# A decoder block with cross-attention and MLP on one core: proj's bias added to the residual by VectorE instead of GpSimd

## The chip, the cores and the metric

The kernel runs on one core of one Trainium2 chip, as one launch. The metric is the device time of that launch in microseconds (us); of several runs the median counts. TensorE is PE in the rows (its weight loads are PEld), VectorE is DVE, ScalarE is ACT, GpSimd is POOL, and SyncE, which only starts transfers here, is SP.

## The reference

Four batches (B = 4) of 512 rows (L) with D = 512 columns, 16 heads, and an MLP 4 x 512 = 2048 wide. Everything is float32.

```python
residual = hidden_states
x = layer_norm(hidden_states, ln1_w, ln1_b)
q = x @ q_w + q_b; k = enc @ k_w + k_b; v = enc @ v_w + v_b      # per head
attn = softmax(where(mask, q @ k.T * scale, min))
out = (attn @ v) @ cproj_w + cproj_b
hidden = out + residual
y = gelu(layer_norm(hidden, ln2_w, ln2_b) @ fc_w + fc_b)
return hidden + (y @ proj_w + proj_b)
```

The last line is what the change touches: `proj_b`, a row of 512 numbers, is added to every row of `hidden`.

## The kernel before, in words

The program is one long list of short steps. A string, `ORDER`, names them in the order in which their instructions are written (`name:batch:part`); each mention of a token runs its generator up to the next `yield`. An engine carries out its own instructions strictly in that written order and waits, at each one, for what it needs from other engines and transfers. Nothing reorders them later, so the string decides what stands behind what in each engine's queue.

The run has two halves. Up to about 545 us attention and MLP steps of the batches are mixed. The rest is the last MLP work of batch 3 and then, for batches 0 to 3, the projection `y @ proj_w`. Each matrix product here is done with sums of blocks so that it takes seven block products instead of eight (and mostly once more inside each of these): blocks are added and subtracted beforehand by VectorE, and results are added up afterwards.

In the projection the steps are these:

- `la` loads gelu's output of a batch from DRAM, where it was parked, into a slot of the tile `swap` (or the two staging tiles `st`), and `gs` (VectorE, lines 331 and 334) forms differences and sums of slots.
- `xs` (VectorE) forms four smaller sums of a slot in the tile `ext`; two such sets alternate. `pt` and `ps` do the same for proj's weights (tiles `pbt`, `ptt`, `mix`, `ys`, `ws`).
- `P` (TensorE, line 637) multiplies them into PSUM banks `acc` and `sc`; `pj` copies the banks into a row tile `xn` (ScalarE, line 663) and adds the second bank (VectorE, `xn<-sc,xn`).
- `hd` (SyncE) loads the parked `hidden` of a batch from the DRAM tensor `xa` in four tiles of 128 rows, t = 0 to 3. For batches 0 and 2 they go to the last slot of `swap`, for batches 1 and 3 to `yT`.
- `pb` (line 738) adds the bias row to the four tiles, one at each mention: `swap<-swap,row` or `yT<-yT,row`, 128 partitions by 512. `row` is proj's bias, loaded once and copied to all partitions.
- `J` adds the results of the products onto the tiles. Mostly this is a transfer that adds as it writes (issued by GpSimd, line 849, `swap<-xn` or `yT<-xn`), for two results of the last batch an addition by VectorE. `so` stores the finished tiles.

For batch 0 the `pb` mentions stand among the last MLP steps, for batches 1 to 3 among the projection steps of the batch before.

Of the kernel before, what the change touches and what calls it, by code (L numbers as in the profile page):

```python
# [241 lines left out]
def xattn_block(ctx: ExitStack, tc: tile.TileContext, x, encT, mask, q_w, k_w, v_w, c_w, w_fc, p_w, vecs, rows, out):  # L242
    nc = tc.nc
# [12 lines left out]
    row = const.tile([P, 2, D], F32, tag="row", name="row")  # L256
# [73 lines left out]
    def add(engine, o, x0, x1):  # L330
        engine.tensor_tensor(o, x0, x1, ALU.add)  # L331
# [403 lines left out]
    def p_bias(b):  # L735
        for t in range(NT):
            o = hids[b % 2][:, t]
            add(nc.gpsimd, o, o, row[:, 0, :])
            yield

    def g_sums(b, n):
# [150 lines left out]
    for _ in range(WARM):  # L892
# [6 lines left out]
        "wk": load_k, "wq": load_q, "wv": load_v, "le": load_enc, "lc": lambda: load(wc, c_w),  # L899
        "pk": prep_k, "q": prep_q, "es": e_sums, "k": kv("k"), "v": kv("v"), "ks": kv_sums("k"), "vs": kv_sums("v"),  # L900
        "kj": k_join, "vj": v_join, "vb": v_bias, "lr": load_row, "pb": p_bias, "qb": q_bias, "m": make_mb,
        "u": scores, "x": exps, "r": turn, "d": stay, "e": exchange, "a": attend,
        "lx": lambda b: load_x((1, b)), "lh": lambda b: load_x((2, b)), "cb": c_bias, "c": cproj,
# [59 lines left out]
```

## Time and profile before

| | us |
|---|---|
| median of 3 runs | 780.06 |
| the 3 runs | 779.04, 780.06, 782.16 |
| time of the profiled execution | 780.34 |
| its span, first to last instruction | 778.3 |
| PE busy in the span | 757.7 (97%) |
| DVE busy | 635.0 (82%) |
| POOL busy | 426.6 (55%) |
| ACT busy | 404.4 (52%) |
| mean granted clock of PE | 0.991 |

The span is what the rows of the trace cover, counted from its first instruction; about 2 us of the execution's time lie around it. A busy share is a mean over both halves. The granted clock is the share of full speed that the chip gave TensorE.

### The profile page before, as it was taken

The numbers are of one execution on the slowest core, as the hardware profiler recorded it, in microseconds if no ns is written. First come the engines' busy times: TensorE is split into PE (matmuls) and PEld (weight loads), VectorE is DVE, ScalarE is ACT, GpSimd is POOL, SyncE is SP. The second block draws the span as 40 slices with busy tenths as digits, with TensorE's granted clock in tenths as the row PEclk, the third lists the DMA queues.
The fourth block names the chain that finished last, engine by engine and source line by source line (L and its number), as shares of the span: only waits on it lengthen the run. The fifth ranks groups of instructions, "written<-read, shape, count | busy, mean of one in ns | idle before, by whom it ended". The sixth has DMA issues, their size and how long they took to land.

```text
span 778.3 us, 14426 instructions
## 1 busy us (share of the span) xinstructions
PE 757.7 (97%) x4990; PEld 555.0 (71%) x4990; DVE 635.0 (82%) x1230; ACT 404.4 (52%) x978; POOL 426.6 (55%) x467
## 2 busy tenths in 40 slices
PE   7999999999999999999999999999999999979898
PEld 4665555556665566766566776758888999979897
DVE  3899999999798799998679696528789797987882
ACT  1668675648879578767847797612333211111110
POOL 3367757956686498556767658726204133431441
PEclk8999999999999999999999999999999999999999
DMA  7578988867876886768778787786545668786456
GB/s 274 169 202 217 252 215 198 236 181 209 242 200 184 247 222 176 221 185 221 210 193 244 228 262 223 205 311 259 156 135 144 218 155 230 136 230 167 109 90 137
DMA packets 69447, 157.48 MB, mean 202 GB/s; under 512 B 11600, under 2 KB 24272, under 8 KB 67712
## 3 DMA queue, kind: packets, MB, share of 16 engines
q1 hardware_dynamic: 54272, 126.72, 56.7%
q0 software_dynamic: 14960, 29.82, 15.2%
q8 instruction: 40, 0.66, 0.4%
q14 instruction: 31, 0.25, 0.1%
q10 hardware_dynamic: 144, 0.02, 0.0%
HBM read 69.23 MB, written 25.17 MB: 121 GB/s over the span
## 4 chain that ended last, share of the span: by engine, by line
PE 69%; DVE 12%; issue 5%; DMA 5%; POOL 4%; ACT 2%; SPq 2%; DVEq 0%; POOLq 0%; ACTq 0%
PE acc L637 27%; PE sc L637 9%; PE acc L467 9%; PE sc L524 7%; PE acc L516 6%; PE acc L582 5%; PE acc L402 5%; SPq L328 2%; DVE ext L334 2%; DVE ptt L532 2%; DVE swap L543 1%; PE acc L370 1%; POOL swap L560 1%; DMA swap<-swap 1%; PE acc L438 1%
## 5 line engine op out<-in xcount | busy, mean ns | idle before, releaser
L535 ACT ACTIVATE ptt<-ptt,mn 128x512 f32<-128x512 f32 x256 | 182.9, 716 | 53.2 <-DVE mn L532 52.1
L532 DVE CUSTOM_DVE_ANT_0 ptt<-sc,mix 128x512 f32<-128x512 f32 x256 | 164.9, 678 | 21.0 <-PE sc L524 17.0
L560 POOL COPY swap<-swap 32x1088 f32<-32x1088 f32 x128 | 140.5, 1098 | 56.4 <-DVE swap L553 45.8
L663 ACT COPY st<-acc 128x256 f32<-128x256 f32 x128 | 46.0, 367 | 103.2 <-PE acc L637 84.3
L663 ACT COPY xn<-acc 128x128 f32<-128x128 f32 x100 | 23.5, 269 | 136.5 <-PE acc L637 134.5
L543 DVE STREAM_TRANSPOSE swap<-ptt 128x1024 f32<-128x1024 f32 x64 | 79.0, 1235 | 9.1 <-DMA swap<-swap 4.5
L524 PE MATMUL sc<-pbt 32*128 32x512 f32 x512 | 78.0, 640 | 0.0
L550 DVE STREAM_TRANSPOSE swap<-ptt 128x1024 f32<-128x1024 f32 x64 | 77.8, 1218 | 0.0
L691 POOL DMA_DIRECT2D gd<-st x32 | 23.7, 741 | 90.7 <-ACT st L689 56.9
L637 PE MATMUL acc<-ys,ws 128*128 128x256 f32 x256 | 65.4, 386 | 0.8 <-ACT st L663 0.7
L582 PE MATMUL acc<-swap,mix 128*32 128x256 f32 x1024 | 61.3, 382 | 0.3 <-ACT ptt L535 0.3
L637 PEld LDWEIGHTS acc<-ys,ws 128*128 128x128 f32 x256 | 46.7, 190 | 18.2 <-issue 4.8
L637 PE MATMUL acc<-yT,pbt 128*128 128x256 f32 x240 | 58.2, 385 | 0.4 <-ACT yT L380 0.4
L516 PE MATMUL acc<-ext,ptt 128*128 128x512 f32 x128 | 58.4, 599 | 0.0
L402 PE MATMUL acc<-mix 128*128 128x512 f32 x128 | 58.1, 598 | 0.0
L637 PEld LDWEIGHTS acc<-yT,pbt 128*128 128x128 f32 x240 | 44.2, 190 | 15.1 <-issue 4.3
L582 PEld LDWEIGHTS acc<-swap,mix 128*32 128x32 f32 x1024 | 30.5, 109 | 30.9 <-issue 10.9
L849 POOL DMA_DIRECT2D swap<-xn x18 | 22.4, 1423 | 50.0 <-ACT xn L663 18.9
L535 ACT ACTIVATION_READ_ACCUMULATOR ptt<-ptt,mn 128x1 f32 x256 | 48.4, 189 | 0.0
L689 ACT ACTIVATE st<-st,vec 128x512 f32<-128x512 f32 x64 | 43.6, 717 | 3.1 <-DVE st L331 2.7
L516 PEld LDWEIGHTS acc<-ext,ptt 128*128 128x128 f32 x128 | 23.5, 190 | 28.6 <-issue 23.5
L402 PEld LDWEIGHTS acc<-mix 128*128 128x128 f32 x128 | 23.6, 190 | 28.4 <-issue 26.3
(154 smaller groups left out, 1609.4 us busy)
## 6 DMA issues: line engine op xcount, KB each, us to landing
swap<-swap SPq DMA_DIRECT2D x384, 136.0 KB, 3.3
gd<-st POOLq DMA_DIRECT2D x32, 512.0 KB, 4.1
swap<-gd SPq DMA_DIRECT2D x12, 1024.0 KB, 5.4
pbt<-fc_w_dram SPq DMA_DIRECT2D x40, 256.0 KB, 3.7
xn<-x_dram SPq DMA_DIRECT2D x32, 256.0 KB, 4.6
ext<-fc_w_dram SPq DMA_DIRECT2D x24, 256.0 KB, 3.0
swap<-xn POOLq DMA_DIRECT2D x18, 256.0 KB, 4.9
ptt<-k_w_dram SPq DMA_DIRECT2D x16, 256.0 KB, 3.5
```

The lines of the kernel that those rows point to most:

```text
L402: nc.tensor.matmul(acc, oT[:, g, ts(t, P)], wc[:, g, :], start=(g == 0), stop=(g == NG - 1))
L467: nc.tensor.matmul(out_, i, j, start=(k + t == 0 and not more), stop=(k == 1), skip_group_check=more or t > 0)
L516: nc.tensor.matmul(acc, S["wq", w][:, d, :], xT[:, d, :], start=(d == 0), stop=(d == ND - 1))
L524: nc.tensor.matmul(sc[h], S["qT", w][r, ts(qt, P)], S["kT", w][r, :], start=True, stop=True)
L532: nc.vector.tensor_tensor_reduce(out=s, in0=sc[h], in1=mb, scale=1.0, scalar=FMAX, op0=ALU.add, op1=ALU.min, accum_out=mn)
L535: nc.scalar.activation(s, s, AF.Exp, bias=mn, scale=-1.0, accum_out=S["sums", w][:, qt, h : h + 1])
L543: nc.vector.transpose(*two_heads[0])
L550: nc.vector.transpose(*two_heads[1])
L560: nc.gpsimd.tensor_copy(pT[ts(i, HD), i], tb[ts(i, HD), i])
L582: nc.tensor.matmul(av[ts(h, HD), : 2 * P].rearrange(shape, **kw), v[:, t, ts(h, HD)], p[t][h], start=(t == 0), stop=(t == NT - 1),)
L637: nc.tensor.matmul(o, x[:, k], w, start=(k == 0 and not more), stop=(k == n - 1), skip_group_check=more)
L663: nc.scalar.copy(g[:, i], S["qa", *key])
```

## The change

The 16 additions of the bias (4 batches of 4 tiles) are issued to VectorE instead of GpSimd. The place of each in the written order stays what it was, so each goes into VectorE's queue between the instructions that are written before and after it.

```diff
     def p_bias(b):
         for t in range(NT):
             o = hids[b % 2][:, t]
-            add(nc.gpsimd, o, o, row[:, 0, :])
+            add(nc.vector, o, o, row[:, 0, :])
             yield
```

The instructions of TensorE, ScalarE and SyncE, and their order, are the same before and after. GpSimd's queue loses the 16 additions and otherwise keeps its order. VectorE's queue gains them. The three pieces below are from VectorE's order, before and after compared; the numbers behind a name tell buffers of one kind apart.

The first place is the end of the last MLP part of batch 3, where proj's weight sums (`ptt`) are formed; the bias goes to tiles 1, 2 and 3 of batch 0.

```order
 L334 TENSOR_TENSOR ws_105<-ws_105,ext 128x256
 L334 TENSOR_TENSOR ptt<-ptt 128x4x128
+L331 TENSOR_TENSOR swap<-swap,row 128x512 x3
 L331 TENSOR_TENSOR xn_83<-sc_74,xn_83 128x2x128
 L334 TENSOR_TENSOR ws_106<-ws_106,ext 128x256
```

Three additions now stand between a weight sum and the addition that empties the PSUM bank sc_74.

The second place is in the projection of batch 2; the bias goes to tiles 1, 2 and 3 of that batch, behind sums of the products' operands (`ext`) and ahead of two differences of slots (`swap<-swap`).

```order
 L334 TENSOR_TENSOR ext<-swap,ext 128x512
 L334 TENSOR_TENSOR ext<-ext,swap 128x512
+L331 TENSOR_TENSOR swap<-swap,row 128x512 x3
 L334 TENSOR_TENSOR swap<-swap 128x1024 x2
 L331 TENSOR_TENSOR xn_87<-sc_76,xn_87 128x2x128
```

Three additions again, ahead of two longer instructions and of the addition that empties sc_76.

The third place is in the projection of batch 3, with the bias of all four tiles of that batch.

```order
 L334 TENSOR_TENSOR ext<-ext,swap 128x512
 L331 TENSOR_TENSOR xn_82<-sc_74,xn_82 128x2x128
+L331 TENSOR_TENSOR yT<-yT,row 128x512 x3
 L331 TENSOR_TENSOR xn_84<-sc_76,xn_84 128x128
 L334 TENSOR_TENSOR swap<-swap,st_88 128x1024
 L334 TENSOR_TENSOR swap<-swap,st_89 128x1024
+L331 TENSOR_TENSOR yT<-yT,row 128x512
 L334 TENSOR_TENSOR ext<-swap,ext 128x512
```

Three additions stand behind a sum of operands and one a little later, behind two differences of slots. The other six go singly into VectorE's queue.

## Rows read from the trace of the kernel before

**Rows 1.** The page: busy time, share of the span, instructions.

```profile
PE 757.7 (97%) x4990; PEld 555.0 (71%) x4990; DVE 635.0 (82%) x1230; ACT 404.4 (52%) x978; POOL 426.6 (55%) x467
```

**Rows 2.** TensorE's waits from 540 us on: total, times, longest.

```profile
PE sc L637 <- DVE ext L334: 3.9, 1, 3.9
PE sc L637 <- DVE xn L331: 2.1, 1, 2.1
PE sc L637 <- DVE st L331: 1.9, 1, 1.9
PE acc L637 <- DVE ws L334: 0.9, 1, 0.9
PE acc L637 <- DVE ext L334: 0.7, 2, 0.5
```

**Rows 3.** Timeline of TensorE: start, duration, instructions, idle time before and its releaser.

```profile
604.23 1.20 PE L637 MATMUL sc<-ys,ext 128*128 128x256 f32 x4 [1.86 <-DVE st L331]
...
699.28 1.16 PE L637 MATMUL sc<-pbt,ext 128*128 128x128 f32 x8 [3.92 <-DVE ext L334]
```

**Rows 4.** Timeline of VectorE.

```profile
552.59 0.69 DVE L331 TENSOR_TENSOR st<-sc,st 128x512 f32<-128x512 f32 x1 [4.26 <-ACT st L663]
...
592.18 4.71 DVE L334 TENSOR_TENSOR ptt<-ptt 128x512 f32<-128x512 f32 x1
...
643.08 0.69 DVE L334 TENSOR_TENSOR ext<-swap 128x512 f32<-128x512 f32 x1
643.68 0.69 DVE L334 TENSOR_TENSOR ext<-ext,swap 128x512 f32<-128x512 f32 x1
...
694.23 5.00 DVE L334 TENSOR_TENSOR ext<-swap 128x512 f32<-128x512 f32 x1
...
700.79 0.69 DVE L334 TENSOR_TENSOR ext<-ext,swap 128x512 f32<-128x512 f32 x1
...
726.83 3.85 DVE L334 TENSOR_TENSOR ext<-swap 128x512 f32<-128x512 f32 x1
...
738.05 3.45 DVE L334 TENSOR_TENSOR ext<-ext,swap 128x512 f32<-128x512 f32 x1
```

**Rows 5.** Timeline of GpSimd in the projection.

```profile
592.50 1.35 POOL L331 TENSOR_TENSOR swap<-swap,row 128x512 f32<-128x512 f32 x1
...
640.30 3.61 POOL L849 DMA_DIRECT2D swap<-xn  x3 [7.60 <-ACT xn L663]
...
694.49 1.72 POOL L331 TENSOR_TENSOR swap<-swap,row 128x512 f32<-128x512 f32 x1
...
696.48 2.18 POOL L331 TENSOR_TENSOR swap<-swap,row 128x512 f32<-128x512 f32 x1
...
727.39 4.38 POOL L331 TENSOR_TENSOR yT<-yT,row 128x512 f32<-128x512 f32 x2
...
737.98 2.96 POOL L331 TENSOR_TENSOR yT<-yT,row 128x512 f32<-128x512 f32 x2
```

**Rows 6.** Bias tile's instructions: cproj's equal addition, duration min/median/max in ns.

```profile
L331 POOL TENSOR_TENSOR xn<-xn,row x16: 1259/1272/1351, 90.8 to 524.5; 128x512 f32<-128x512 f32 x16
```

**Rows 7.** Windows: length, PE, PEld, DVE, ACT, POOL busy, granted clock, DMA share, GB/s.

```profile
600.00:620.00 20.00, 18.14 (x129) 17.25 (x129) 15.33 (x24) 5.21 (x15) 2.66 (x3) 0.91 0.60 211
...
700.00:720.00 20.00, 20.00 (x167) 20.00 (x167) 14.52 (x25) 2.83 (x13) 2.38 (x2) 0.91 0.63 163
```

**Rows 8.** Timeline of ScalarE.

```profile
601.55 0.37 ACT L663 COPY st<-acc 128x256 f32<-128x256 f32 x1 [2.28 <-PE acc L637]
```

**Rows 9.** Line 849 at 546 us: the first adding transfer, and its landing.

```profile
L849 POOL DMA_DIRECT2D swap<-xn x1: 1243/1243/1243, 546.5 to 546.5; - x1
...
DMA to landing us min/median/max: 5.5/5.5/5.5
```

**Rows 10.** Loads of `xa` from 540 us on: issue to landing of all 14.

```profile
DMA to landing us min/median/max: 2.5/3.2/6.7
```

**Rows 11.** Timeline of SyncE: the load of tile 3 of batch 2.

```profile
683.36 0.77 SPq L328 DMA_DIRECT2D swap<-xa  x1
```

## The prediction

> **What bounds the kernel now.** I read the page first: TensorE is busy 97% of the span, VectorE 82% [rows 1]. So a change can give back only what TensorE waits for or loses to its clock, and it can cost whatever it makes TensorE wait. All 16 additions lie behind 540 us, so I then asked for TensorE's waits from there on. There are six, 9.5 us together, and each ends with VectorE: 3.9, 2.1, 1.9, 0.9 and two of 0.7 together [rows 2]. In this half VectorE is the engine that is late. Two of the six are long, 1.86 us up to 604.23 and 3.92 us up to 699.28 [rows 3].
>
> Next: why is VectorE late there? In its timeline most instructions of 128 by 512 take 0.69 us, and back to back they start 0.60 us apart (643.08, 643.68). But four rows of the same size take 4.71, 5.00, 3.85 and 3.45 us [rows 4]. GpSimd's timeline beside them shows what these have in common. The bias additions at 694.49 and 696.48 lie inside the VectorE row that began at 694.23 and ended at 699.23, just where TensorE's longest wait ended. The pair at 727.39 lies over the row of 726.83, the pair at 737.98 over that of 738.05, and the addition at 592.50, with a second one right behind it, over that of 592.18 [rows 4, 5]. What they do not share is a transfer: while GpSimd issued three in a row at 640.30, VectorE's rows at 643.08 and 643.68 kept their 0.69 us [rows 4, 5]. So I read it thus: while GpSimd adds, VectorE's two-input addition stands still.
>
> The third thing TensorE loses is clock. In the 20 us around each long wait the mean granted clock is 0.91, because it falls to the lower level, 1.2 of 2.4 GHz, for a few us after the pause [rows 7]. That is 20 x 0.09 = 1.8 us at each place, 3.6 us together.
>
> **What is removed.** Four VectorE rows give back 4.71 + 5.00 + 3.85 + 3.45 less 4 x 0.69, that is 14.25 us for eight additions, 1.8 us each [rows 4].
>
> An equal addition, cproj's bias on GpSimd, takes 1.27 us at the median [rows 6]; eight of that length would be 10.2 us, so the rows lose 4 us more than the additions' own length explains. I put all of it down to the additions, since at 694 VectorE did not move on between two that follow closely. If the surplus has another cause, it stays: that is a rival below.
>
> "SBUF — State Buffer" of the Trainium skill, section "Who interferes with whom", says: a VectorE instruction with two SBUF inputs and a GpSimd instruction that reads SBUF exclude each other, and the second to issue waits until the first has finished. That the two exclude each other agrees with the rows; that one instruction costs the other at most its own length is less than the rows of 4.71 and 5.00 us show [rows 4].
>
> **What is added.** Sixteen additions of 128 by 512 on VectorE. The trace before has the same shape from the same memory at a pitch of 0.60 us [rows 4], so 9.6 us of VectorE's time if none finds an idle stretch, and none if all do. For the eight additions above, 4.8 us go in where 14.25 come out. What hides an addition is that TensorE is then supplied ahead: over most of the projection it does not wait at all although VectorE works without a gap. Where that cover is gone, each costs its 0.60.
>
> *The three at 592 us* follow a row that ends 4.02 us sooner, cost 1.8, and leave VectorE 2.2 us ahead on its way to the addition that ended the wait at 604.23. That is more than the wait of 1.86.
>
> *The three behind 700.79* follow a row that ends 4.31 us sooner [rows 4]. They need tile 3, loaded at 683.36; at the longest landing of such a load, 6.7 us, it is there at 690.1 [rows 10, 11], over 10 us ahead of its place. *The four of batch 3* follow relief of 3.16 and 2.76 us and cost 2.4.
>
> *The first one* is the least covered. It must wait for the transfer that adds onto the same tile, issued at 546.5, 1.24 us long in issue and landing after 5.5 [rows 9]: at 552.0 if that counts from the start, at 553.2 from the end of the issue. VectorE's next instruction began at 552.59 after 4.26 us idle [rows 4]. So the addition, 0.60 long, delays what follows by 0 to 1.2 us; I take 0.6 as the one addition that shows.
>
> **The sum.** TensorE's waits, 9.5, and its lost clock, 3.6, make 13.1 us. Of this a little stays. At 604.23 the addition that TensorE waited for also needs ScalarE's copy, which ends at 601.92 [rows 8]; with 0.69 behind it TensorE can go on at 602.6, while its pause began at 602.37, so 0.3 stays. At 699.28 the sum could be ready at 694.9, before the pause began at 695.36. Taking 0.3 and the 0.6 of the first addition away leaves 12.2 us. The profiled execution took 780.34 us, so this gives 768.1; it lies 0.28 above the median of 780.06, so the median should be about **767.9 us**.
>
> **The rivals.**
>
> *Relief, but part of the waits comes back.* Once VectorE is early, something behind it ends last: ScalarE's copies, a load, or additions that pile up (three in a row are 1.8 us). For it: VectorE works nearly without a gap in much of the projection, so small margins there are not seen in the trace. Against it: TensorE does not wait in those stretches. If half of the six waits stays, 4.8, and with it one of the two falls of the clock, 1.8, the time is 767.9 + 6.6 = 774.5; if the clock falls once more and nothing else, 769.7. I take 769.9 to 775 as this case.
>
> *Only the additions' own length comes back.* With 1.27 us each, the two additions at 592 give VectorE back 2.5 us and the three in its own queue take 1.8, which leaves 0.7 of the 1.86 that it needs at 604.23; at 699.28 it has 2.5 of the 3.92 back. So 1.1 and 1.4 us of waiting stay (0.3 of it is in the sum already), and with pauses that long the falls of the clock may stay too, 3.6: 767.9 + 2.2 + 3.6 = 773.7. By the skill's rule above, each addition giving back no more than its own length, this is the case to expect. Against it: no other GpSimd work that could hold VectorE lies in those stretches, and the transfers at 640.30 did not [rows 4, 5].
>
> *The change doesn't do what it says, and ends slower.* The stretched rows could be due to something that runs in the same stretches, such as the adding transfers, and GpSimd's additions would be only neighbours. Then VectorE keeps its long rows and gets 9.6 us of work. The place that decides is 592 to 604: three additions come ahead of a wait in which TensorE already stands, so 1.8 us go straight to the end; with the three of the third place and the first addition it is 4.2 (1.8 + 1.8 + 0.6), and 9.6 if nothing hides any. That is 784 to 790. It decides where an addition gives back less than its 0.60 us. Against it: the transfers at 640.30 slow nothing [rows 4, 5].
>
> *Transfers block VectorE's queue.* On GpSimd an addition that waits for its tile holds up few; on VectorE all sums for TensorE stand behind it. For it: the tiles come by loads that take 2.5 to 6.7 us [rows 10]. Against it: the margin of over 10 us at the second place. A load would have to be later by that margin and by 12 us more before the gain is gone; the time would be 776 to 784.
>
> *More than the sum.* If all six waits go and nothing shows, 780.06 less 13.1 is 767.0; below 766 something outside these waits would have to help.
>
> **How the numbers follow.** The forecast, 766 to 769.9: 0.60. Part of the waits comes back, 769.9 to 775: 0.18, of which I put 0.14 below 773.5. Only the additions' own length, 771.5 to 774.5: 0.07, of which 0.05 below 773.5. No relief: 0.05. Blocked by transfers: 0.05, mostly without a measurable change. Below 766: 0.05. The likeliest case gives the predicted time. A range of 765.5 to 773.5 holds 0.60, 0.14, 0.05 and about 0.03, so 8 in 10. About 0.5%, 3.9 us, is what a measurement of this kernel can tell from no change: faster takes the first three cases and the last, 0.90; same 0.05; slower 0.05.
>
> **What would show it.** Right: no VectorE row of 128 by 512 above 1 us in the projection; VectorE's new `row` additions at about 0.69 us; its busy time lower, although it has 16 instructions more; TensorE's waits on VectorE from 540 us on below 2 us instead of 9.5, and a granted clock of 1.00 in the stretches of both long waits. Wrong: rows of 3 to 5 us that stay on VectorE would speak for the rival without relief; a VectorE wait of some us ahead of a `row` addition, released by a transfer, for the one with transfers; TensorE waiting at new places for ScalarE or a load, or a clock that still falls, for the first; rows of 1.5 to 3 us beside no addition, for the second. The prediction fails on its size if TensorE's waits go and as much comes back within the next 20 us.

## The result, and the profile after

| | before | after |
|---|---|---|
| median in the same comparison, us | 779.55 (4 runs, 777.69 to 782.16) | 767.18 (4 runs, 766.04 to 768.09) |
| profiled execution, us | 780.34 | 766.04 |
| its span, us | 778.3 | 764.3 |
| PE busy, DVE busy, POOL busy in the span, us | 757.7, 635.0, 426.6 | 753.0, 620.0, 404.5 |
| mean granted clock of PE | 0.991 | 1.000 |

The ratio after to before is 0.9838, with a 95% interval of 0.9806 to 0.9871: the change makes the kernel 1.6% faster. The forecast was 767.9 us, with a range of 765.5 to 773.5. A second comparison of the same two kernels gave 767.14 us and a ratio of 0.984 (0.9814 to 0.9865).

The page of the changed kernel, its first part, answers to [rows 1]:

```profile
PE 753.0 (99%) x4990; PEld 551.6 (72%) x4990; DVE 620.0 (81%) x1246; ACT 404.1 (53%) x978; POOL 404.5 (53%) x451
```

VectorE does 16 instructions more, 1246 instead of 1230, and is busy 15.0 us less. This one line already says that GpSimd's additions cost VectorE more time than it now spends doing them itself.

TensorE's waits from 530 us on (total, times, longest), which answer to [rows 2]:

```profile
PE sc L637 <- DVE xn L331: 0.7, 1, 0.7
```

Of six waits with 9.5 us one is left, and it is a new one: its place is 740.06 in the span. The four additions for batch 3 (three from 727.52, one at 731.80, 2.4 us together) now stand ahead of the addition to `xn` in a stretch that VectorE works through almost without a gap.

The instances of the 16 moved additions (duration min/median/max in ns, first and last start):

```profile
L331 DVE TENSOR_TENSOR swap<-swap,row x8: 682/684/686, 579.9 to 692.2; 128x512 f32<-128x512 f32 x8
...
L331 DVE TENSOR_TENSOR yT<-yT,row x8: 681/683/685, 613.3 to 731.8; 128x512 f32<-128x512 f32 x8
```

All 16 take 0.68 us. VectorE's timeline at the places of the four long rows of [rows 4]:

```profile
589.87 0.69 DVE L334 TENSOR_TENSOR ptt<-ptt 128x512 f32<-128x512 f32 x1
590.47 1.89 DVE L331 TENSOR_TENSOR swap<-swap,row 128x512 f32<-128x512 f32 x3
...
688.13 0.69 DVE L334 TENSOR_TENSOR ext<-swap 128x512 f32<-128x512 f32 x1
...
691.00 1.89 DVE L331 TENSOR_TENSOR swap<-swap,row 128x512 f32<-128x512 f32 x3
...
714.93 0.69 DVE L334 TENSOR_TENSOR ext<-swap 128x512 f32<-128x512 f32 x1
...
723.82 0.68 DVE L334 TENSOR_TENSOR ext<-ext,swap 128x512 f32<-128x512 f32 x1
...
727.18 0.42 DVE L331 TENSOR_TENSOR xn<-sc,xn 128x256 f32<-128x256 f32 x1 [2.69 <-ACT xn L663]
727.52 1.89 DVE L331 TENSOR_TENSOR yT<-yT,row 128x512 f32<-128x512 f32 x3
```

The rows of 4.71, 5.00, 3.85 and 3.45 us are now 0.69, 0.69, 0.69 and 0.68. Behind them three additions take 1.89 us together, and no row of `row` additions waits for a transfer.

The windows of both long waits (length, PE, PEld, DVE, ACT, POOL busy, granted clock, DMA share, GB/s), moved by the time gained; compare [rows 7]:

```profile
600.00:620.00 20.00, 20.00 (x166) 19.59 (x165) 16.55 (x30) 5.75 (x17) 2.73 (x3) 1.00 0.82 274
680.00:700.00 20.00, 20.00 (x182) 20.00 (x181) 13.87 (x26) 3.07 (x13) 3.92 (x4) 1.00 0.80 223
```

The clock is 1.00 in both, against 0.91, and TensorE does not pause. TensorE's instruction that waited 1.86 us at 604.23 [rows 3] now starts 3.57 us earlier, and without idle time:

```profile
600.66 1.03 PE L637 MATMUL sc<-ys,ext 128*128 128x256 f32 x4
```

Followed along equal TensorE instructions, the lead grows in steps: 0.4 us at 566 (ahead of all that the change does there, so a difference between two executions), 5.3 at 608.61, 11.9 at 704.58, 14.1 at 732.72, 14.9 at 741.55. The 0.7 us wait then takes some back, and the spans differ by 14.0. The steps from 604 to 608 and around 699 hold most of it. From that instruction at 566 to the end, the windows' row of the kernel before and that of the changed kernel (columns as above) are:

```profile
566.00:778.30 212.30, 199.07 (x1573) 192.34 (x1571) 169.59 (x248) 38.69 (x134) 64.54 (x53) 0.98 0.63 161
```

```profile
565.61:764.30 198.69, 194.30 (x1573) 188.91 (x1571) 153.64 (x263) 38.79 (x134) 42.94 (x38) 1.00 0.68 172
```

The same 1573 matmuls take 13.6 us less. 4.8 of it is TensorE's busy time, and 8.8 its idle time (13.2 less 4.4), which is the 9.5 of the six waits less the new 0.7. Where the busy time went is seen in the two stretches around the long waits, from one TensorE instruction to another that are equal in both kernels (columns as above). The kernel before:

```profile
601.56:609.39 7.83, 5.97 (x32) 5.41 (x30) 7.03 (x10) 0.53 (x2) 0.13 (x1) 0.78 0.71 268
695.09:705.92 10.83, 6.92 (x47) 6.72 (x46) 9.06 (x8) 0.85 (x4) 3.58 (x3) 0.84 0.46 108
```

The changed kernel:

```profile
600.02:604.09 4.07, 4.07 (x31) 3.89 (x30) 2.36 (x4) 0.52 (x2) 0.00 (x0) 1.00 0.98 356
689.00:694.02 5.02, 5.02 (x47) 5.02 (x46) 4.99 (x9) 0.85 (x4) 1.74 (x2) 1.00 0.32 134
```

TensorE is busy 1.9 us less in each, 3.8 together: that is the lower clock. The other 1.0 us lies outside these two stretches, where the windows of both kernels show a clock of 1.00. The medians are 12.4 apart: the profiled execution after is 1.1 us faster than its median, and the one before 0.8 slower.

### The profile page after: what moved, and what is told of

It is laid out like the page before. It is cut to its first block, busy times and chain, and to the rows that moved or that the text cites. A ratio compares the mean times of both kernels' runs of the same rounds, so it can differ in the third digit from the quotient of the medians.

```text
span 764.3 us, 14415 instructions
## 1 busy us (share of the span) xinstructions
PE 753.0 (99%) x4990; PEld 551.6 (72%) x4990; DVE 620.0 (81%) x1246; ACT 404.1 (53%) x978; POOL 404.5 (53%) x451
## 4 chain that ended last, share of the span: by engine, by line
PE 73%; DVE 9%; POOL 6%; issue 4%; DMA 3%; ACT 2%; SPq 2%; DVEq 0%; POOLq 0%; ACTq 0%
PE acc L637 31%; PE sc L637 11%; PE acc L467 8%; PE sc L524 7%; PE acc L516 6%; PE acc L582 5%; PE acc L402 4%; DVE ptt L532 2%; SPq L328 2%; POOL swap L560 2%; PE acc L370 1%; DVE swap L543 1%; DVE xn L363 1%; DMA pbt<-fc_w_dram 1%; DVE swap L550 1%
```

## The experiments

Two theories were to be told apart. The one of the forecast: GpSimd's addition, because it reads from SBUF, makes VectorE's two-input instructions stand still, VectorE is then late for TensorE at few places, and the clock falls there. Its rivals: the additions are only neighbours of whatever stretches the rows (the queue of GpSimd, its transfers, its writes); or VectorE's new work is hidden by nothing and the gain is something else. All times are medians, with lowest and highest behind them, and each ratio is to the kernel before on the same chip. The diffs are against the changed kernel.

**Without the additions.** What do the 16 additions still cost on VectorE?

```diff
             o = hids[b % 2][:, t]
-            add(nc.vector, o, o, row[:, 0, :])
             yield
```

> The 16 bias additions are left out altogether, so the output lacks proj's bias. Theory (GpSimd's additions held VectorE, and the moved ones are covered): as the changed kernel, 767.2, within 1 us, since VectorE's additions are hidden. Rival (the moved additions show): up to 16 x 0.60 = 9.6 us below, 757.6; if only one shows, 766.6.

Measured: 765.62 us (764.65 to 766.3), ratio 0.9804 (0.9781 to 0.9826). TensorE does not wait at all from 540 us on, and VectorE is busy 610.2 us. So 16 additions with 9.8 us of busy time cost about 1.6 us (767.18 less 765.62; against the kernel with fills, two experiments below and on the same chip, 1.5; by the ratios 2.7; the two intervals overlap, so it is a small cost rather than a sure one). The theory had expected less than 1 us. Everything that this addition could give back by going elsewhere is this small cost.

**GpSimd adds as well.** VectorE keeps the bias, and GpSimd adds two rows into a tile that nobody uses, at the same places.

```diff
             add(nc.vector, o, o, row[:, 0, :])
+            add(nc.gpsimd, row[:, 1, :], row[:, 0, :], row[:, 0, :])
             yield
```

> The changed kernel, and GpSimd does at each place an addition of the same size on the bias rows alone (two SBUF inputs, into a dead buffer), which nobody waits for. Theory (a GpSimd instruction that reads SBUF holds VectorE's two-input rows): long VectorE rows of 1.5 to 5 us come back and with them most of the waits and both falls of the clock, 777 to 783, since VectorE also keeps the 16 additions. Rival (the long rows were due to something beside the additions, or the gain came from the residual being ready sooner): 767, no VectorE row above 1 us.

Measured: 771.79 us (770.65 to 774.67), ratio 0.9894 (0.9859 to 0.9928). VectorE's busy time is back to 634.9 us, 14.9 more, although it has the same instructions. Its timeline shows the long rows again:

```profile
591.71 2.22 DVE L334 TENSOR_TENSOR ptt<-ptt 128x512 f32<-128x512 f32 x1
...
682.97 2.38 DVE L334 TENSOR_TENSOR ext<-swap,ext 128x512 f32<-128x512 f32 x1
...
719.58 2.13 DVE L334 TENSOR_TENSOR ext<-swap 128x512 f32<-128x512 f32 x1
...
728.90 2.00 DVE L334 TENSOR_TENSOR ext<-ext,swap 128x512 f32<-128x512 f32 x1
```

TensorE's waits in it, from 530 us on:

```profile
PE sc L637 <- DVE xn L331: 1.9, 3, 1.0
PE acc L637 <- DVE ws L334: 0.9, 2, 0.6
```

Two more have 0.8 and 0.6 us.

The direction is as expected, the size was not: 4.6 us instead of some 10 to 16. The 15 us on VectorE are there, but as 16 pieces that fall mostly where TensorE is supplied ahead: the longest wait is 1.0 us and the mean clock stays at 0.999. GpSimd's two additions of the place with the wait of 3.92 us have moved: they now start at 696.47 and 698.25, behind VectorE's own three (from 694.42), beside two differences of slots that take 5.08 us instead of 2.35, and TensorE has no long wait there. What an addition costs VectorE and what that costs the span are two things.

**GpSimd writes only.** The same, with a fill instead of an addition.

```diff
             add(nc.vector, o, o, row[:, 0, :])
+            nc.gpsimd.memset(row[:, 1, :], 0.0)
             yield
```

> As e2, but GpSimd only writes: it fills the same dead buffer of 128 x 512 with zeros. Theory in the narrow form (what excludes is the reading of SBUF): no long VectorE rows, 767 within 1 us. Rival one (any GpSimd instruction on SBUF holds VectorE): long rows by the length of the fill, some us above 767. Rival two (the gain came from GpSimd's queue being free for its transfers): slower too, but without long VectorE rows.

Measured: 767.13 us (766.49 to 768.5), ratio 0.9826 (0.9803 to 0.985), on the same chip as the run above. The fills (duration min/median/max in ns):

```profile
L739 POOL MEMSET row<- x16: 525/990/1980, 561.5 to 725.7; 128x512 f32 x16
```

They are as many, in the same queue at the same places, write as much and take a median of 0.99 us. VectorE is busy 619.2 us, without a long row beside them. Here is the place that had the row of 3.85 us, with transfers being issued as before, in GpSimd's timeline and in VectorE's:

```profile
714.24 3.63 POOL L850 DMA_DIRECT2D swap<-xn  x3 [7.13 <-DVE ext L334]
716.42 2.56 POOL L739 MEMSET row<- 128x512 f32 x2
```

```profile
715.90 0.69 DVE L334 TENSOR_TENSOR ext<-swap 128x512 f32<-128x512 f32 x1
716.50 0.68 DVE L334 TENSOR_TENSOR ext<-ext,swap 128x512 f32<-128x512 f32 x1
```

So GpSimd's queue, its transfers and its writes are not the cause; with the additions of the run above, the reading is. That rules out the rival in which the additions were only neighbours.

**GpSimd copies.** Between the two: one input is read, one output written.

```diff
             add(nc.vector, o, o, row[:, 0, :])
+            nc.gpsimd.tensor_copy(row[:, 1, :], row[:, 0, :])
             yield
```

> As e2, but GpSimd reads one SBUF input instead of two: it copies the 128 x 512 bias rows into the dead buffer at each place. Theory (reading SBUF excludes, for as long as GpSimd's instruction lasts): VectorE rows longer by about the copy's length, and a time between those of e3 (767.1) and e2 (771.8), 768 to 770. Rival (only two inputs on GpSimd exclude): 767.1, no VectorE row of 128 x 512 above 1 us.

Measured: 767.45 us (766.0 to 772.12), ratio 0.9856 (0.9829 to 0.9883). VectorE is busy 627.3 us, 7.3 more than in the changed kernel, with rows like these in its timeline:

```profile
681.27 1.43 DVE L334 TENSOR_TENSOR ext<-swap,ext 128x512 f32<-128x512 f32 x1
682.63 1.08 DVE L334 TENSOR_TENSOR ext<-ext,swap 128x512 f32<-128x512 f32 x1
```

The copy of 681.56 to 683.16 lies over both, and they lose 0.74 and 0.39 us. One input is enough to hold VectorE up, by about half of what an addition does (0.46 against 0.93 us each, 7.3 and 14.9 over 16); the copies are also shorter (median 1.12 us against 1.51), and how much of the half is due to that was not separated. On the span it shows nothing: 767.45 against 767.14 for the changed kernel on the same chip (below). The expected 1 to 3 us did not come.

**VectorE adds twice.** How much more fits under the cover?

```diff
             add(nc.vector, o, o, row[:, 0, :])
+            add(nc.vector, row[:, 1, :], o, row[:, 0, :])
             yield
```

> The changed kernel with each bias addition done twice on VectorE, the second into a dead buffer: 9.6 us more for VectorE. Theory (VectorE's additions are covered because TensorE is supplied ahead): 767 to 769. Rival (the cover is used up by the first 16, VectorE is the bound): up to 767.2 + 9.6 = 776.8, with TensorE's waits on VectorE back at the places where three stand in a row.

Measured: 772.27 us (772.03 to 772.56), ratio 0.989 (0.9868 to 0.9912). The second 16 cost 5.1 us, the first 16 some 1.6. TensorE's waits from 530 us on:

```profile
PE acc L637 <- DVE ext L334: 1.5, 2, 1.1
PE sc L637 <- DVE xn L331: 1.4, 3, 0.7
PE acc L637 <- DVE swap L334: 0.8, 1, 0.8
```

Three more have 0.6, 0.5 and 0.4 us. The theory's expectation (767 to 769) failed here, and the time lies inside the rival's (up to 776.8): what the second 16 cost says that the first 16 had used up a good part of the lead. The waits sum to 5.2 us, 4.5 more than in the changed kernel, which is nearly the whole 5.1; none is above 1.1, and the clock stays at 1.000.

**One batch at a time on GpSimd.** The change undone for the four additions of batch 0, 1, 2 or 3 alone, in four kernels.

```diff
-            add(nc.vector, o, o, row[:, 0, :])
+            add(nc.gpsimd if b == 0 else nc.vector, o, o, row[:, 0, :])
```

> Only batch 0's four additions stay on GpSimd, the other twelve on VectorE. From the shift of equal TensorE instructions between the two traces at this place (1.0 us at 567, 3.9 around 604): theory 767.2 + 4.9 = 772.1, with the wait before 604 back and the clock below 1.00 in the 20 us behind it. Rival (the waits of the kernel before were one chain in which each came from the one ahead): 767 or, on the other side, near 780.

> Only batch 1's four additions stay on GpSimd. From the shift at its places (0.4 at 658, nothing at the other three): theory 767.6, not to be told from 767.2, though VectorE keeps four rows lengthened by 1 to 2 us. Rival (a lengthened VectorE row always costs): 767.2 + 4 x 1.2 = 772.

> Only batch 2's four additions stay on GpSimd. From the shift at its place (6.3 us between 694 and 705): theory 773.5, with one VectorE row near 5 us, one TensorE wait near 4 us and the clock below 1.00 behind it. Rival (one chain): 767 or near 780.

> Only batch 3's four additions stay on GpSimd. From the shift at its places (2.2 at 731, 0.8 at 741, 0.85 given back later): theory 769.4. Rival (one chain): 767 or near 780. By the theory the excesses of the four kernels over 767.2 add up to the whole, 12.4; by the rival they don't.

| on GpSimd | us | ratio | above 767.18 |
|---|---|---|---|
| batch 0 | 770.71 (769.17 to 771.3) | 0.9887 (0.9857 to 0.9916) | 3.5 |
| batch 1 | 768.33 (764.43 to 768.85) | 0.9848 (0.9811 to 0.9885) | 1.1 |
| batch 2 | 773.25 (772.4 to 775.55) | 0.9924 (0.9901 to 0.9947) | 6.1 |
| batch 3 | 768.99 (767.81 to 772.25) | 0.9876 (0.9834 to 0.9919) | 1.8 |

The four sum to 12.5 us, and the whole change is 12.4; by the ratios it is 14.3 against 12.6. That they agree so well is in part luck, since a median holds all that an execution lost, elsewhere too. The profiled executions can be compared over one stretch instead: from the TensorE instruction that starts at 565.61 in the changed kernel to the one at 740.06. At its start the four kernels are already 2.3, 1.9, 1.7 and 0.8 us behind the changed kernel. Over the stretch each takes this much longer than the changed kernel does; the last column is by how much the changed kernel's lead grew at that batch's place (from 0.4 us to 5.3, 5.7, 11.9 and 14.1):

| | from | to | longer, us | the same place in the kernel before |
|---|---|---|---|---|
| changed kernel | 565.61 | 740.06 | | |
| batch 0 on GpSimd | 567.92 | 744.58 | 2.2 | 4.9 |
| batch 1 on GpSimd | 567.54 | 742.40 | 0.4 | 0.4 |
| batch 2 on GpSimd | 567.29 | 748.84 | 7.1 | 6.2 |
| batch 3 on GpSimd | 566.36 | 743.01 | 2.2 | 2.2 |
| kernel before | 566.00 | 754.16 | 13.7 | 13.7 |

The four parts make 11.9 of 13.7 us. Batches 1 and 3 cost alone what they cost in the whole; batch 0 costs less and batch 2 somewhat more. Batch 2 shows the long wait whole. Its VectorE timeline and TensorE's:

```profile
689.82 5.00 DVE L334 TENSOR_TENSOR ext<-swap 128x512 f32<-128x512 f32 x1
...
694.87 1.44 PE L637 MATMUL sc<-pbt,ext 128*128 128x128 f32 x5 [3.92 <-DVE ext L334]
```

GpSimd's timeline in the same kernel:

```profile
689.30 1.20 POOL L849 DMA_DIRECT2D swap<-xn  x1 [6.22 <-DMA st<-gd]
690.08 1.72 POOL L331 TENSOR_TENSOR swap<-swap,row 128x512 f32<-128x512 f32 x1
691.29 1.68 POOL L849 DMA_DIRECT2D yT<-xn  x1
692.07 2.19 POOL L331 TENSOR_TENSOR swap<-swap,row 128x512 f32<-128x512 f32 x1
```

And the window around it:

```profile
680.00:700.00 20.00, 16.09 (x123) 15.89 (x122) 16.47 (x16) 1.40 (x6) 7.45 (x6) 0.85 0.72 213
```

The row of 5.00 and the wait of 3.92 are back to the hundredth as in [rows 3 to 5], and the clock falls again (0.85 here, 0.98 in the next 20 us). 3.9 of wait and 20 x 0.17 = 3.4 of clock make 7.3, near the 7.1 of the table; in this execution the clock falls for longer than it did in the kernel before (0.91 in 20 us), and that covers the 0.9 us by which batch 2 alone costs more.

Batch 0 brings back a row of 4.70 us (594.11), but TensorE waits only 0.78 at the instruction that stood at 604.23, and 0.9 at an earlier one, and the clock is 1.00 there. The rest of the wait of 1.86 in the kernel before came from batch 1. Its first addition on GpSimd lay over two differences of slots just ahead of the addition that TensorE waited for; VectorE's row and GpSimd's in the kernel before:

```profile
599.35 3.43 DVE L334 TENSOR_TENSOR swap<-swap 128x1024 f32<-128x1024 f32 x2
```

```profile
600.04 1.66 POOL L331 TENSOR_TENSOR yT<-yT,row 128x512 f32<-128x512 f32 x1 [3.70 <-DMA yT<-xa]
```

With batch 0 alone on GpSimd the same pair takes 2.35:

```profile
601.27 2.35 DVE L334 TENSOR_TENSOR swap<-swap 128x1024 f32<-128x1024 f32 x2
```

The pair is 1.08 us shorter, and so is the wait (1.86 less 0.78). So of the 4.9 us of this place 1.1 of wait and the fall of the clock (1.9) came only where both batches were on GpSimd. Batch 1 alone does not show them, since VectorE is ahead there: the pair runs at 596.81, GpSimd's addition at 600.83. Batch 0's own share is 2.2 us, not the 4.9 expected and not the 3.5 of the median. What else this profiled execution lost lies ahead of the additions: among it a fall of the clock at 306 us, where the changed kernel has none. The window in this kernel and, below it, in the changed one:

```profile
306.00:308.00 2.00, 2.00 (x7) 1.63 (x6) 2.00 (x8) 1.21 (x5) 2.00 (x3) 0.50 0.00 0
```

```profile
306.00:308.00 2.00, 2.00 (x12) 1.68 (x12) 2.00 (x8) 2.00 (x8) 2.00 (x3) 1.00 0.00 0
```

Batch 1 has rows of 2.54 and 1.76 us on VectorE that cost TensorE next to nothing (one wait of 0.2): 1.1 us in the median, inside what runs differ by, and 0.4 over the stretch. Batch 3 brings back rows of 3.83 and 3.45 and the waits of 2.06 and 0.53 of before, with no fall of the clock.

**The changed kernel again.** The same kernel once more, for a measure of how far two comparisons agree.

> The changed kernel once more, beside the next one on the same chip: 767.2 within 0.8.

Measured: 767.14 us (765.64 to 767.93), ratio 0.984 (0.9814 to 0.9865), with the one wait of 0.7 us. The two comparisons agree to 0.04 us.

**The additions in VectorE's idle stretches.** Nine of the 16 mentions of `pb` are moved in the order to places where VectorE idles; one of five moves:

```diff
-P:1:7 pt:2 pj:1:6 P:1:6 xs:1:7
+P:1:7 pt:2 pj:1:6 P:1:6 la:2:7 hd:1 pb:1 xs:1:7
...
-P:1:7 P:1:2 la:2:7 hd:1 pb:1 xs:1:2
+P:1:7 P:1:2 xs:1:2
```

> The changed kernel with nine of the 16 additions written earlier, into stretches in which VectorE waited for TensorE or ScalarE in the changed kernel's trace (before 649, 654, 672, 684 and 727 us); the order of the other engines and queues is the same. Theory (what the moved additions still cost, 767.2 less the 765.6 without any, comes from additions that stand in VectorE's way): 765.8 to 766.5. Rival (the cost is not where these nine stand, or the new places wait for loads): 767.2 or above.

Measured: 768.28 us (763.65 to 768.32), ratio 0.9844 (0.9817 to 0.9872). In the profiled execution TensorE does not wait from 540 us on, and its span is 761.9 us, but that is the fastest of five executions, and the median is not below the changed kernel's 767.14. The expected 765.8 to 766.5 was missed, and it is not shown to be better. There was at most the small cost of the first experiment to win.

## Why the prediction was right

**What bounds it.** VectorE was the engine that was late, and its lateness came from GpSimd's reading. This step was only read from neighbouring rows beforehand; the fill, the copy and the added additions show it by taking the queue, the writes and the reads apart. The reading that ruled out transfers was weaker than it looked: beside each of the four long rows GpSimd was issuing a transfer too (at 593.71, 693.71, 725.18 and 737.20 in the kernel before). It is the run with fills, with the same transfers and no long row, that rules them out.

**The relief.** The claim was that the whole stretch of each row, 14.25 us over four, goes with the additions, and not only their own length. All four rows are down to 0.69 or 0.68. VectorE's busy time supports the size: 635.0 plus 16 x 0.60, less 620.0, is 24.6 us given back by 16 additions, 1.5 each, of the same order as the 1.8 taken for the eight beside the long rows. What was misread is the surplus of 4 us over the additions' own length. It came from taking 1.27 us for each; in their own rows the eight last 14.4 us (1.35 and 1.83 at 592, 1.72 and 2.18 at 694, 4.38 and 2.96 for the pairs at 727 and 738), which is all of the 14.25. The additions are longer at these places, and most of them start while GpSimd is still issuing the transfer ahead of them.

**The waits and the clock.** 13.1 us were to go, 9.5 of waits and 3.6 of clock. From 566 on 8.8 of idle time and 4.8 of busy time went: the waits as priced, 3.8 of clock in the two stretches that the forecast named, and 1.0 of busy time elsewhere that was not in the sum. That it is these that count, and not VectorE's time as such, is what the batches show: batch 2 alone gives 6.1 us, while batch 1, with lengthened rows that TensorE hardly waits for, gives 1.1, which is not measurable. One wait had a second cause that the forecast did not see: of the 1.86 at 604.23, 1.08 came from batch 1's addition at 600.04, and only the rest from batch 0's at 592. It made no difference to the forecast, since all 16 additions moved. That the median fell by 12.4 us where 12.2 were forecast is closer than the runs can tell: the profiled pair lies 14.3 apart.

**The small terms.** Two of them were wrong in their place, and that their sum of 0.9 is near the 0.7 us of wait that did come is luck. The 0.3 at 604 hung on the wrong copy of ScalarE's. In the changed kernel VectorE's addition runs at 597.88, behind the copy of 597.41 and ahead of the next one, which starts at 600.00 and is the one that stood at 601.55; ScalarE's timeline there and VectorE's:

```profile
600.00 0.37 ACT L663 COPY st<-acc 128x256 f32<-128x256 f32 x1 [2.22 <-PE acc L637]
```

```profile
597.88 0.68 DVE L331 TENSOR_TENSOR st<-sc,st 128x512 f32<-128x512 f32 x1
```

The first addition was put at VectorE's gap at 552, with 0.6 of cost. There the timeline after shows the row with the same 4.26 us of idle time and nothing new behind it, and the addition stands later:

```profile
552.20 0.69 DVE L331 TENSOR_TENSOR st<-sc,st 128x512 f32<-128x512 f32 x1 [4.26 <-ACT st L663]
...
579.33 0.68 DVE L334 TENSOR_TENSOR ptt<-pbt,ptt 128x512 f32<-128x512 f32 x1
579.93 0.68 DVE L331 TENSOR_TENSOR swap<-swap,row 128x512 f32<-128x512 f32 x1
```

It waits there for nothing, since the transfer it needs had landed some 27 us before. The mistake was to look for the place by the wait that it should have, instead of by the instruction that stands ahead of it in the order. What came instead is the 0.7 at 740.06, at the additions of batch 3, which the forecast had taken as covered.

**The rivals.** *Part of the waits comes back* holds for 0.7 us of 9.5. *Transfers block VectorE's queue*: no `row` addition waits; instead GpSimd's transfers wait for VectorE's additions, and TensorE has no wait at these places. One of the two:

```profile
692.28 1.20 POOL L849 DMA_DIRECT2D swap<-xn  x1 [11.98 <-DVE swap L331]
```

*No relief* is excluded by the rows. *Only the additions' own length* was priced with 1.27 us each, and the time it gave, 773.7, did not come. With the length of their own rows there is little left between it and the forecast: with batch 2 alone on GpSimd the two additions take 1.72 and 2.19 us, 3.91, and VectorE's row loses 4.31; it does not finish in the 0.27 us between them, in which GpSimd is issuing a transfer (691.29, 1.68 us), and ends 0.56 behind the second. "SBUF — State Buffer" of the Trainium skill, section "Who interferes with whom", says that VectorE's two-input instruction contends with GpSimd instructions that read SBUF and not with ones that only write it. The runs agree on both halves: VectorE's busy time rises by 14.9 us with additions, by 7.3 with copies, and with fills it does not rise (619.2 against 620.0). The prediction held the rows of 4.71 and 5.00 us against a wait of at most one instruction's length; each of these rows lay over two additions, so only what goes beyond both is left, 0.40 us here.

**What GpSimd still does.** The longest remaining VectorE row of this shape behind 540 us confirms the reading by work that the change left alone. VectorE's row, and GpSimd's timeline beside it, in the changed kernel:

```profile
543.21 2.39 DVE L334 TENSOR_TENSOR yT<-yT 128x512 f32<-128x512 f32 x1
```

```profile
543.56 0.81 POOL L334 TENSOR_TENSOR ws<-ext,ws 128x256 f32<-128x256 f32 x1
544.24 0.81 POOL L334 TENSOR_TENSOR ws<-ws,ext 128x256 f32<-128x256 f32 x1
545.12 1.07 POOL L334 TENSOR_TENSOR ws<-ext,ws 128x256 f32<-128x256 f32 x1
```

VectorE's row is 1.70 us too long, about as much as the first two additions last (1.62). It ends at 545.60, 0.55 behind the second and inside the third, which takes 1.07 where the others take 0.81. So here VectorE did get in ahead of the next addition. Whether moving these as well would pay was not tried.

What stays open: the 1.0 us of busy time outside the two falls of the clock, why the clock fell for longer with batch 2 alone, and why some of GpSimd's additions last up to 3.15 us where an equal one takes 1.27.

## What to carry to other kernels

Work moved to GpSimd is not free for VectorE when it reads SBUF beside VectorE's two-input instructions: here each such addition took about 1.5 us from VectorE, and the same addition in VectorE's own queue takes 0.60. A wait that goes can have had two causes: undo a change in parts before putting a price on each. Look for instructions of one shape with very different durations, lay the other engine's timeline over them, and price the move by the waits of the engine that bounds, not by busy time: GpSimd's reading left VectorE some 15 us busier than in the changed kernel in two arrangements, of which 12.4 showed in the time in the kernel before and 4.6 in the one in which GpSimd adds as well. And the cover is finite: the first 16 additions cost some 1.6 us, the next 16 cost 5.1.

## What the runs showed of the hardware that was not expected

- Whether VectorE gets in between two GpSimd additions differs. At 694.23 in the kernel before, and again with batch 2 alone, it did not in the 0.27 us between their rows, in which GpSimd was issuing a transfer: its 0.69 us row took 5.00. At 543.21 in the changed kernel it did, with 0.07 us between the second and the third.
- The row that begins first is not the one that proceeds: VectorE's began at 689.82, GpSimd's addition at 690.08, and it was VectorE's that took 5.00 us. GpSimd's row begins inside the issue of a transfer (689.30, 1.20 us), so its start need not be the start of its reading.
- A GpSimd copy, with one input, holds VectorE up by about half as much as an addition (7.3 us against 14.9 over 16; the copies are shorter, 1.12 us against 1.51), a fill not at all.
- The granted clock of TensorE was 0.91 (before) and 0.85 (batch 2 alone) in the 20 us around waits of 3.92 us, and 0.91 around the one of 1.86. With batch 3 alone the wait of 2.06 left no mark (the mean over that run is 1.000), and with batch 0 alone the one of 0.78 left none either. The length of a wait alone does not tell whether the clock falls.
- Some falls have nothing to do with the change: 0.50 at 306 us with batch 0 alone, some 250 us ahead of the additions. No DMA engine moved anything there, but neither did one in the changed kernel, whose clock was 1.00; TensorE had idled 0.5 us from 298 to 302, where the changed kernel has no idle time.
